# Query projections of a second self attention by sets of seven block products

## The chip, the cores and the metric

The kernel runs on one core of a Trainium2 chip. Its metric is the device time of one execution in microseconds (us). The kernel before took 1819.48 us, the median of three runs from 1816.45 to 1821.72. All data is 32-bit floating point.

The core has five engines that work beside each other: TensorE for matmuls (PE in the profile, its weight loads as PEld), VectorE (DVE), ScalarE (ACT), GpSimd (POOL) and SyncE (SP), which here only issues transfers. Matmul results land in PSUM banks; all other tiles lie in SBUF.

## The reference

The computation is a two-layer decoder over 8 sequences of 112 tokens with 512 features (896 tokens). Each layer has a self attention, a cross attention to a context of 375 tokens, and a feed-forward part, each on the layer norm of the running sum `x` and added to it. The change touches the self attention of the second layer:

```python
q = q * cos + _rotate_half(q) * sin
k = k * cos + _rotate_half(k) * sin
...
scores = jnp.einsum('bhqd,bhkd->bhqk', q, k) * scale
...
attn = jax.nn.softmax(scores, axis=-1)
out = jnp.einsum('bhqk,bhkd->bhqd', attn, v)
out = out.transpose(0, 2, 1, 3).reshape(b, s, H * DH)
return out @ Wo.T
```

Here `q = x @ Wq.T` has 16 heads of 128 features, `k` and `v` 4 heads, each used by four query heads. The positions run over each sequence's 112 tokens. The mask of this attention leaves out keys more than 128 positions ahead, which no pair here is.

## The kernel before, in words

`self_attention(1, ...)` works in eight turns, one for each pair of a key head group `g` (0 to 3) and a half `hf` of the tokens (448 tokens, four sequences). The input `xT[hf]` lies transposed: 128 features on the partitions, four chunks of features, 448 tokens. For each turn, `prepare(n)` gives a list of steps: the keys (`roped` with `wk`) and the four query heads of the group (`roped` with the group's 512x512 matrix `matrices[g][0]`). Each such head is four matmuls of 128x128 by 448 columns, which the profile shows as eight records, into one PSUM bank of the tag `mm`, which has two buffers.

`roped` then copies the bank to a tile `raw` (L630 on DVE, L632 on ACT in the first layer), has SP move its two halves of 64 rows crosswise into a tile `turned` (L637), multiplies `raw` by the cosine on POOL (L639) and `turned` by the sine on DVE (L640), and adds both on POOL into `qT` or `kT` (L641). `raw` and `turned` have three buffers each.

`scores` (L695) makes a unit's 16 score matmuls, `softmax` takes the maxima on DVE (L466), the exponentials on ACT (L469) and scales on POOL (L476); `contexts` transposes the result (L487, copied out by DVE at L488), multiplies it with the values (L714) and copies it to `oT` on ACT (L719). `pipeline` and `weave` set the order: while a turn's first unit is worked on, `weave` mixes in the next turn's keys and queries, then the output projection of the turn before (`outputs(n - 1, True)`); with the second unit it mixes in `outputs(n, False)` and then the steps of `extra(n)`. The order on PE is the written one; the other engines' instructions are ordered by a planner that keeps the dependencies and lets an instruction go early when its inputs are ready.

The output projection adds into `x`, which keeps tiles of 128 tokens. Where a turn completes two tiles and `g` is below 3, `out_pair` makes both together: the two tiles' tokens, the matrix's columns and the 512 inner features are each cut in two, and seven products of the 2x2 blocks (`sevens`, numbered 1, 6, 2 and 5, 7, 3, 4 in the order that PE makes them) take the place of eight. They need three sums of input blocks, made per pair by `block_sums` (L253 to L258, the tile `os`), and three differences of matrix blocks, made per matrix by `block_differences` (L267 to L272, the tile `wos`, and one in place in `wo`). The step `lay` in `prepare` makes the latter. One half of a seven uses two banks, and a product that adds to a bank waits until the engine that reads the bank has read the product before. The readers (`put`, L768 and L771 on DVE, L782 and L785 on POOL) keep three differences in a tile `od`. `os`, `od` and `wos` have one buffer each in a pool `dq`.

Weights come through the pool `wpool` of six buffers of 1 MB. The second layer's first two query matrices are fetched at the start, the third in `prepare(3)` and the fourth in `prepare(5)`.

## Time and profile before

The profile is of one execution that took 1820.96 us; its span, from the first to the last instruction, is 1819.0 us.

| engine | busy us | share of the span | instructions |
|---|---|---|---|
| PE | 1769.6 | 97% | 7150 |
| PEld | 989.8 | 54% | 7150 |
| DVE | 952.1 | 52% | 1692 |
| ACT | 627.5 | 34% | 1906 |
| POOL | 770.0 | 42% | 673 |

| in the second self attention, 930 to 1190 us | count | mean |
|---|---|---|
| query matmul record, 448 columns | 224 | 540 ns |
| output product record, 256 columns | 252 | 379 to 394 ns |
| DVE copy of a raw head (L630) | 35 | 625 ns |
| DVE sine product (L640) | 35 | 620 ns |
| POOL cosine product of a query head (L639) | 28 | 1439 ns |
| POOL sum of a query head (L641) | 29 | 1142 ns |
| DVE reader of an output product (L768) | 54 | 414 to 421 ns |

A record's duration of a matmul runs until its last result; the next one is issued before that. So the pace of PE is read from the distance of the starts, or from the chain of waits, and not from these means. In the timeline, the brackets give how long the engine stood idle before an instruction and what ended that. The chain of waits is followed back from the last instruction; a piece names the work that the end of the program hung on at that time.

### The profile page before, as it was taken

To read this page: it belongs to the slowest core of one execution; us is meant where nothing else is said; L and a number is where in the kernel's file an instruction comes from. 1 tells how busy PE (TensorE), PEld (TensorE's weight loads), DVE (VectorE), ACT (ScalarE), POOL (GpSimd) and SP (SyncE) were. 2 spreads that over 40 slices of the span, in tenths; PEclk is the share of its full clock that TensorE was granted. 3 is DMA by queue.
4 is the path that set the end of the run, shared out by engine and by line. 5 is a ranking of instruction groups with operands and counts; after the bars stand their busy time and mean duration, and the time that the engine had idled before them with its cause. 6 is when DMAs were issued, how large, how long until landed. Compare 5 with 4: busy or idle time off the path is not lost.

```text
span 1819.0 us, 20344 instructions
## 1 busy us (share of the span) xinstructions
PE 1769.6 (97%) x7150; PEld 989.8 (54%) x7150; DVE 952.1 (52%) x1692; ACT 627.5 (34%) x1906; POOL 770.0 (42%) x673
## 2 busy tenths in 40 slices
PE   8999999999999999999999999999999999999998
PEld 4454544555454555567655666645654444554444
DVE  4455666645454544786543545536755444344444
ACT  2444444554333434375221221236722111031110
POOL 3464555355656550000135666512353354434533
PEclk9999999999999999999999999999999999999999
DMA  6132423143133212011121222300011212011111
GB/s 242 27 118 64 143 82 89 58 150 115 48 85 101 58 52 93 24 70 63 63 66 33 75 77 44 104 18 1 8 37 53 75 55 81 23 50 55 63 34 41
DMA packets 40429, 124.50 MB, mean 68 GB/s; under 512 B 7332, under 2 KB 20700, under 8 KB 32904
## 3 DMA queue, kind: packets, MB, share of 16 engines
q1 hardware_dynamic: 33192, 93.73, 16.0%
q0 software_dynamic: 6848, 29.36, 5.4%
q8 instruction: 56, 0.92, 0.2%
q14 instruction: 45, 0.37, 0.1%
q10 hardware_dynamic: 288, 0.12, 0.0%
HBM read 94.56 MB, written 10.28 MB: 58 GB/s over the span
## 4 chain that ended last, share of the span: by engine, by line
PE 81%; DVE 8%; POOL 4%; ACT 3%; DMA 2%; issue 1%; SPq 1%; ACTq 0%; POOLq 0%; DVEq 0%
PE pr_q L244 10%; PE pf L244 5%; PE po_x L1004 4%; PE pb_dn L1550 4%; PE po_at L442 3%; PE pv L244 3%; PE po_at L446 3%; PE pr_k L244 3%; PE ps L695 3%; PE pq_x L244 3%; PE po L714 3%; PE po_x L442 2%; PE po_x L446 2%; PE pa_dn L1550 2%; PE ps_x L968 2%; PE pb_up L1550 2%
## 5 line engine op out<-in xcount | busy, mean ns | idle before, releaser
L244 PE MATMUL pr_q<-xT_at,wq 128*128 128x448 f32 x512 | 204.1, 543 | 0.0
L244 PEld LDWEIGHTS pr_q<-xT_at,wq 128*128 128x128 f32 x512 | 93.8, 190 | 84.3 <-issue 81.3
L469 ACT ACTIVATE p<-p,nmax 112x113 f32<-112x113 f32 x256 | 95.8, 376 | 109.7 <-DVE nmax L466 108.8
L1733 POOL TENSOR_TENSOR h<-silu,h 128x448 f32<-128x448 f32 x64 | 73.9, 1157 | 122.2 <-ACT silu L1731 122.0
L476 POOL TENSOR_TENSOR p<-p,total 112x896 f32<-112x896 f32 (+1 forms) x56 | 85.3, 1529 | 93.7 <-DVE total L472 86.5
L244 PE MATMUL pf<-h,sw 128*128 128x448 f32 x256 | 106.0, 540 | 0.0
L1127 POOL TENSOR_SCALAR tl<-tr,ternary_bounds 128x512 f32<-128x512 f32 x32 | 51.8, 1618 | 123.2 <-DMA tr<-in_c_w_dram 123.2
L1735 DVE TENSOR_TENSOR h<-h,share 128x448 f32<-128x448 f32 x48 | 41.5, 871 | 111.9 <-POOL h L1733 111.9
L974 DVE TENSOR_REDUCE nmax_x<-ps_x 112x2 f32<-112x750 f32 x64 | 57.1, 933 | 79.4 <-PE ps_x L968 79.4
L641 POOL TENSOR_TENSOR qT<-qT,turned_q 128x448 f32<-128x448 f32 x64 | 75.5, 1182 | 51.3 <-DVE turned_q L640 42.0
L639 POOL TENSOR_TENSOR qT<-raw_q,tables 128x448 f32<-128x448 f32 x64 | 85.1, 1334 | 27.9 <-DVE raw_q L630 20.4
L1004 PE MATMUL po_x<-pT_x,kv 125*128 125x448 f32 x192 | 89.2, 549 | 1.6 <-DVE pT_x L999 1.3
L976 ACT ACTIVATE p_x<-ps_x,nmax_x 112x375 f32<-112x375 f32 x124 | 69.7, 574 | 38.2 <-DVE nmax_x L974 38.1
L1550 PE MATMUL pb_dn<-h,sums_dn 128*128 128x448 f32 x192 | 80.3, 541 | 1.0 <-DVE acc L1772 0.5
L1731 ACT ACTIVATE silu<-pf,cols 128x448 f32<-128x448 f32 x64 | 40.5, 633 | 117.9 <-PE pf L244 117.0
L488 DVE COPY pT<-ppt 112x448 f32<-112x448 f32 x96 | 57.1, 617 | 43.5 <-PE ppt L487 43.5
L469 ACT ACTIVATE p<-ps,nmax 112x112 f32<-112x112 f32 x128 | 43.2, 366 | 101.7 <-DVE nmax L466 101.7
L244 PEld LDWEIGHTS pf<-h,sw 128*128 128x128 f32 x256 | 48.9, 191 | 48.2 <-issue 41.7
L442 PE MATMUL po_at<-wo,oT 128*128 128x512 f32 x152 | 74.3, 611 | 0.0
L446 PE MATMUL po_at<-wo,oT 128*128 128x512 f32 x152 | 71.4, 592 | 0.0
L719 ACT COPY oT<-po 128x448 f32<-128x448 f32 x64 | 31.9, 525 | 104.9 <-PE po L714 104.9
L476 POOL TENSOR_TENSOR p_e<-p_e,total_e 112x896 f32<-112x896 f32 x16 | 26.9, 1682 | 96.5 <-DVE total_e L472 72.2
(357 smaller groups left out, 3941.5 us busy)
## 6 DMA issues: line engine op xcount, KB each, us to landing
tw<-in_c_w_dram SPq DMA_DIRECT2D x16, 512.0 KB
tr<-in_c_w_dram POOLq DMA_DIRECT2D x32, 256.0 KB, 3.8
signs<-tl POOLq DMA_DIRECT2D x32, 256.0 KB, 2.9
fup<-in_f_up_dram SPq DMA_DIRECT2D x8, 1024.0 KB
fdn<-in_f_dn_dram SPq DMA_DIRECT2D x8, 1024.0 KB
turned_q<-raw_q SPq DMA_DIRECT2D x128, 56.0 KB
turned_q<-raw_q SPq DMA_DIRECT2D x64, 112.0 KB
share<-gated SPq DMA_DIRECT2D x12, 448.0 KB
```

The lines of the kernel that those rows point to most:

```text
L244: nc.tensor.matmul(ps, lhsT, rhs, start=(k == 0), stop=(k == len(pairs) - 1))
L442: nc.tensor.matmul(ps[0], lhsT, rhs, start=(c == 0), stop=False)
L446: nc.tensor.matmul(ps[0], lhsT, rhs, start=False, stop=(c == len(pairs) - 1))
L469: nc.scalar.activation(p[:, h, :], src[:, h, :], AF.Exp, bias=nmax[:, h : h + 1], accum_out=total[:, h : h + 1])
L476: spread[:] = [nc.gpsimd.tensor_tensor(p[:, at, :T], p[:, at, :T], total[:, at], ALU.mult).ins]
L488: copied[:] = [nc.vector.tensor_copy(kept["pT"][:, 4 * k : 4 * k + 4, :], pt[:T, :, :T]).ins]
L639: nc.gpsimd.tensor_tensor(by_batch(dst), by_batch(raw), cos, ALU.mult)
L641: nc.gpsimd.tensor_tensor(dst, dst, turned, ALU.add)
L976: e = nc.scalar.activation(p[:, 2 * j + s, :], ps[:T, s, :L], AF.Exp, bias=nmax[:, s : s + 1], accum_out=total[:, 2 * j + s : 2 * j + s + 1],)
L1004: nc.tensor.matmul(po[0][:, : 4 * T], kv[:, b, c, :], pTs[c], start=(c == 0), stop=(c == NLC - 1))
L1550: nc.tensor.matmul(bank[n], lhsT, rhs, start=(k == 0 and n in (1, 6, 7)), stop=(k == len(pairs) - 1), skip_group_check=True,)
L1733: nc.gpsimd.tensor_tensor(to, s, at["h1"][:, c, half(hf)], ALU.mult)
```

## The change

From the third turn on, the four query heads of a turn are made as two pairs, each by a set of seven products. The two heads of a pair are one cut, the halves of the 512 inner features the second, and two halves of 224 tokens the third. `paired` makes a pair in two steps. The three sums of matrix blocks, with one difference in place, are made per matrix (`add_up`, for matrices 1 to 3), the four differences of input blocks once per token half (`differ`); both are steps of `extra`: the first matrix's sums and the first half's differences in turn 0, the second half's in turn 1, the other matrices' in turns 2 and 4.

The end of `roped` becomes a function `rotated`, whose last add can go to DVE; the second head of the second pair uses that. The raw copies of the first two turns go to ACT. The output pairs' `os` and `od` move from `dq` to the three buffers of 512 columns with the tag `xn` in the pool of the normed inputs: the first two input sums in one buffer, the third sum and the first difference in another, the other two differences in the third. In `dq` their place is taken by `sums` (one buffer) and `xs0`, `xs1`.

```diff
@@ extra
-                return [(3.4, lambda b=b: values(b)) for b in range(first, last)]
+                steps = [(3.4, lambda b=b: values(b)) for b in range(first, last)]
+                if not l0 and n == 0:
+                    more = later(add_up(1) + differ(0))
+                    steps = [*more[:3], steps[0], *more[3:6], steps[1], *more[6:]]
+                return steps
             if not l0:
-                return []
+                g, hf = turns[n]
+                return later(differ(1) if n == 1 else add_up(g + 1) if hf == 0 and g + 1 < G else [])
@@ roped
-            if bias is None:
-                nc.vector.tensor_copy(raw, ps[:, :HT])
+            raw = new_raw(name)
+            if bias is None and name.startswith("k") and xs:
+                nc.vector.tensor_copy(raw, ps[:, :HT])
+            elif bias is None:
+                nc.scalar.copy(raw, ps[:, :HT])
...
+        def differ(hf):
+
+            b = xT[hf].rearrange("p (h k) (s t) -> p h k s t", h=2, s=2)
+
+            def new():
+                xs[hf] = dq[0].tile([P, 4, 2, HT // 2], F32, tag=f"xs{hf}", bufs=1, name=f"xs_{layer}_{hf}")
+
+            return block_differences(
+                (nc.vector, nc.gpsimd), new, lambda k: xs[hf][:, k],
+                b[:, 0, :, 0], b[:, 0, :, 1], b[:, 1, :, 0], b[:, 1, :, 1],
+            )
+
+        def add_up(g):
+
+            a = matrices[g][0].rearrange("p (h k) (c m n) -> p h k c m n", h=2, c=2, m=2)
+
+            def new():
+                sums[g] = dq[0].tile([P, 3, 2, 2, P], F32, tag="sums", bufs=1, name=f"sums_{layer}_{g}")
+
+            return block_sums(
+                (nc.vector, nc.gpsimd), new, lambda k: sums[g][:, k],
+                a[:, 0, :, :, 0], a[:, 1, :, :, 0], a[:, 0, :, :, 1], a[:, 1, :, :, 1],
+            )
+
+        def paired(turn, qT, c, nm):
...
+            def put(n, ps):
+                if n == 1:
+                    raw[:] = [new_raw(f"q_{nm}_{2 * c + m}") for m in range(2)]
+                r0, r1 = raw
+                add = lambda to, of: nc.vector.tensor_tensor(to, of, ps, ALU.add)
+                if n == 1:
+                    nc.vector.tensor_copy(r0[:, tok[1]], ps)
+                elif n == 6:
+                    add(r1[:, tok[0]], r0[:, tok[1]])
+                elif n == 2:
+                    nc.scalar.copy(r0[:, tok[0]], ps)
+                elif n == 5:
+                    add(r1[:, tok[1]], r1[:, tok[0]])
+                elif n == 7:
+                    add(r1[:, tok[1]], r1[:, tok[1]])
+                elif n == 3:
+                    add(r0[:, tok[1]], r1[:, tok[0]])
+                    rotated(qT[:, 2 * c, :], r0, "q", f"q_{nm}_{2 * c}")
+                else:
+                    add(r1[:, tok[0]], r1[:, tok[0]])
+                    rotated(qT[:, 2 * c + 1, :], r1, "q", f"q_{nm}_{2 * c + 1}", nc.vector if c else nc.gpsimd)
+
+            first, second = sevens(products, put, half_, f"q_{nm}_{c}", c == 1)
+            return [(2.3, first), (3.0, second)]
+
+        def rotated(dst, raw, which, name, last=nc.gpsimd):
...
-            nc.gpsimd.tensor_tensor(dst, dst, turned, ALU.add)
+            last.tensor_tensor(dst, dst, turned, ALU.add)
@@ prepare
-            more = later(lay(g - 1)) if not l0 and n and hf == 0 else []
-            for c in range(4):
-                steps += more[c : c + 1]
-                steps.append((3.0, lambda c=c: roped(
...
+            if l0 or n < 2:
+                for c in range(4):
+                    steps.append((3.0, lambda c=c: roped(
...
+            else:
+                more = [step for c in range(2) for step in paired(n, qT, c, nm)]
+                if hf == 0:
+                    more = [step for pair in zip(more, later(lay(g - 1))) for step in pair]
+                steps += more
@@ out_pair, add_up
-                    s.append(dq[0].tile([P, 3, 2, P], F32, tag="os", bufs=1, name=f"os_{nm}"))
+                    pair = [npool.tile([P, D], F32, tag="xn", bufs=3, name=f"os_{nm}_{k}") for k in range(2)]
+                    d.append(pair[1][:, D // 2 :])
+                    pair = [t.rearrange("p (s c n) -> p s c n", s=2, c=2) for t in pair]
+                    s.extend([pair[0][:, 0], pair[0][:, 1], pair[1][:, 0]])
...
@@ out_pair, put
-                    d.append(dq[0].tile([P, 3, D // 2], F32, tag="od", bufs=1, name=f"od_{nm}"))
-                d1, d2, d3 = (d[0][:, m] for m in range(3))
+                    d.append(npool.tile([P, D], F32, tag="xn", bufs=3, name=f"od_{nm}"))
+                d1, d2, d3 = d[0], d[1][:, : D // 2], d[1][:, D // 2 :]
```

## The prediction

> **What bounds the kernel now.** I read the page's busy times first, then the chain of waits cut to the second self attention (about 930 to 1190 us), then the timeline around each gap that the chain shows.
>
> ```profile
> PE 1769.6 (97%) x7150; PEld 989.8 (54%) x7150; DVE 952.1 (52%) x1692; ACT 627.5 (34%) x1906; POOL 770.0 (42%) x673
> ...
> PE 81%; DVE 8%; POOL 4%; ACT 3%; DMA 2%; issue 1%; SPq 1%; ACTq 0%; POOLq 0%; DVEq 0%
> ```
>
> PE is busy 97% of the span, and the chain runs through it. So a microsecond of matmul taken from this stage is worth one, unless PE then waits. One turn of the stage in the chain (start, length, what):
>
> ```profile
> 1055.46 3.02 PE pr_q L244 x8
> 1058.87 3.02 PE pr_q L244 x8
> 1061.89 1.50 PE po L714 x4
> 1063.40 3.01 PE pr_q L244 x8
> 1066.41 0.86 PE px_at_True L286 x4
> 1067.27 0.98 PE py_at_True L286 x4
> 1068.26 0.86 PE px_at_True L286 x4
> 1069.12 0.86 PE py_at_True L286 x4
> 1069.98 0.86 PE pz_at_True L286 x4
> ```
>
> A query head is eight records in 3.01 to 3.02 us, 377 ns each at 448 columns. The output sets are already made of seven products: four records of 256 columns in 0.86 us, 216 ns each. One product has 0.98, because its bank still waited for the raw copy of the last head. Busy time of the engines in such a stretch (window, length, PE, PEld, DVE, ACT, POOL):
>
> ```profile
> 1049.00:1072.00 23.00, 23.00 (x80) 13.69 (x79) 10.95 (x22) 3.76 (x18) 15.65 (x13) 1.00 0.33 83
> 1072.00:1085.00 13.00, 12.49 (x76) 10.36 (x75) 7.61 (x17) 3.76 (x18) 7.74 (x9) 1.00 0.25 104
> ```
>
> The clock is 1.00; DVE and POOL have room on the mean. The second stretch holds the one repeated gap, seen in the timeline (start, length, engine):
>
> ```profile
> 1005.94 1.09 DVE L466 TENSOR_REDUCE nmax<-ps 112x8 f32<-112x896 f32 x1 [0.46 <-PE ps L695]
> 1006.39 1.26 POOL L785 TENSOR_TENSOR x<-x,od_at_True 128x512 f32<-128x512 f32 x1
> 1006.62 1.03 PE L286 MATMUL py_at_False<-wos,os_at_False 128*128 128x256 f32 x4
> ...
> 1007.68 0.42 DVE L771 COPY od_at_False<-px_at_False 128x256 f32<-128x256 f32 x1 [0.65 <-PE py_at_False L286]
> 1008.16 1.13 PE L286 MATMUL px_at_False<-wo,oT 128*128 128x256 f32 x4 [0.52 <-DVE od_at_False L771]
> ```
>
> PE should have gone on at 1006.62 + 0.865 = 1007.48 and starts at 1008.16. DVE was free from 1007.03, yet the copy into od started only when POOL's L785, which reads the previous od tile, ended at 1007.65.
>
> **The change, part by part.**
>
> *Shorter products.* Six turns have two head pairs each: 12 pairs. A pair was 16 records, 16 x 0.377 = 6.03 us. It becomes seven products of two matmuls, 28 records of 224 columns. From 377 ns at 448 and 216 ns at 256 columns the slope is 0.839 ns a column, so 224 columns take 189 ns: 28 x 0.189 = 5.30 us. That is -0.73 a pair, **-8.8 us**. The weight load (190 ns as shown) should not stand in the way: the score matmuls of 112 columns go 16 in 1.57 us, 98 ns each, each with its own load of 112 columns.
>
> *Bank wait gone.* The pair ends with a reader of 224 columns in place of one of 448. DVE copies out of PSUM took 0.625 us at 448 and 0.424 at 256, so 0.39 at 224. The 0.12 us in the first py product of the six late output pairs goes: **-0.7 us** (ends 0 and -0.7).
>
> *The output sets move into the xn buffers.* The first difference now lies in the tile of the third input sum, no longer in the tile that L785 reads. The copy can start when nmax ends, 1007.03, ends at 1007.45, and PE starts near 1007.5. Next in line is then nmax itself, which just fits. The gap of 0.68 us comes three times: up to -2.0, at worst 0; I take **-1.6**.
>
> *Waits inside the new sevens.* A product's reader starts 0.20 us after its last record has been issued (998.87 to 999.07), runs 0.39, and PE follows 0.05 later: 0.64 us. The one product between covers 0.757. The margin is 0.12 us, where the output sets had 0.865 - 0.67 = 0.20. Laid out over one turn from the end of the key matmuls: the key's rotated half lands near 3.8 us, so its sine product (0.62) falls between the readers of products 5 and 7, and product 4 starts some 0.15 late. The pT copies (0.62 each) meet the gap behind a half set. The sine products of the first pair fall into the 1.5 us of po between the halves of the second. A raw buffer is reused at the sixth product of the second pair, 0.5 us before its transfer out has ended; DVE waits there, but PE has product 2 and po ahead of the next bank it needs. Ends: 0, as in the late output pairs apart from the bank wait, and 0.68 a seven, the worst repeated gap. I take 0.25, nearer to the first, since that is the same scheme: 12 x 0.25 = **+3.0** (0 to +8.2). DVE gets, per pair, six readers for two copies, 6 x 0.39 - 2 x 0.625 = +1.1 us, and in every second pair the last add (0.62): +2.8 us a turn on 10.95 of 23. POOL loses one add of 1.13 a turn, ACT gains two short copies in a time when its exponentials are over.
>
> The Trainium skill, "SBUF — State Buffer", section "Who interferes with whom", speaks against the new DVE work: a DVE instruction with both inputs in SBUF and a GpSimd one that reads SBUF exclude each other for a whole instruction. The trace agrees in part: wos L271 took 1.65 us beside POOL's L785 against 0.66 where it started first, but the sine products stayed at 0.62 while POOL ran. By the rule alone 18 new instructions of that kind (6 of the differences, 6 sums, 6 adds) could each wait about 1 us; were all on the path, that would be +18 us.
>
> *Input differences and the first sums.* They are ready from about 926 us on. DVE stands idle 2.34, 1.61 and 3.76 us in 932 to 944, which hides them (8 instructions of about 0.65, and four on POOL); if one comes earlier, POOL may be in a sum of 1.27 us (the row of L270) when the first scores wait for qT at 928.83. Ends 0 and +1.3; I take **+0.4**.
>
> *Sums of the third and fourth matrix.* Each has two DVE instructions (0.68, or 1.65 beside POOL) and two of 1.27 on POOL. They must follow the last product that uses the sums before, so they fall beside the late output pair, where the gaps of DVE are 0.44. Ends 0 and 1.65 each; I take 0.4 each, **+0.8**. The matrix itself is fetched at 1000.11, 40 us before: no wait.
>
> *Ten raw copies on ACT.* Around 910.5 a raw copy holds DVE 0.53 us ahead of rest_h, on the chain; on ACT it would stand before top_h instead. Ends -0.5 and +0.6; I take **-0.2**.
>
> *Last heads into the scores.* Both heads of the second pair come out within 0.8 us. The later one: reader, transfer (2.96 us in the row at 1030.18 to 1033.14), sine product 0.62, add on DVE 0.62, about 4.9 us after the last product. The output pair behind it runs 6.1, so 1.2 is left (0.1 today): **0**. With no output pair behind it, it would cost all of 4.9. SP's queue carries the same count of transfers, the two of a pair closer together.
>
> Sum: -8.8 - 0.7 - 1.6 + 3.0 + 0.4 + 0.8 - 0.2 = **-7.1 us**. The profiled execution took 1820.96 us (span 1819.0), which would be 1813.9; it stands 1.5 above the median of 1819.48. I carry the difference to the median: 1812.4 us.
>
> The Trainium skill, "VectorE: DVE Perf Modes", section on the errata of SBUF-source operations, asks for pieces of 512 elements or more, since each instruction pays a fixed cost. Here the fixed part is 0.625 - 448 x 1.05 ns = 0.155 us in the rows; by it the cut into 224 costs 12 x 4 x 0.155 = 7.4 us of DVE, which would end the gain only if DVE were the bound.
>
> **The rivals.**
>
> *A. The readers eat the gain.* Every new seven loses what the early output pair loses now, 0.68 us: 12 x 0.68 = 8.2 in place of 3.0, so -7.1 + 5.2 = -1.9: 1817.6 us. For it: the margin of 0.12. Against it: in the late output pairs DVE kept step with a sine product in between.
>
> *B. Slower: DVE sets the pace of the sevens.* A two-input SBUF instruction held by POOL (1.65 us) or a wait for a rotated half (2.40 us of DVE idle at 1063.16 to 1065.56) stands ahead of a reader in each seven. The other terms sum to -10.1, so B decides from 10.1 / 12 = 0.84 us a seven; at 1.65 less the margin, 1.5, it gives -10.1 + 18 = +8: 1827 us. Against it: the sine products are not stretched by POOL (at most 0.77 us), and that DVE wait had nothing ready behind it.
>
> *C. The products don't get shorter.* If a record of 224 columns took the 216 ns of one of 256, a pair would be 6.05 us, no gain, and the sum -7.1 + 9.0 = +1.9: 1821.4 us. Against it: the 98 ns records.
>
> **How the numbers follow.** About 0.3% (5.5 us) is what a measurement of this kernel can tell from no change: faster is below 1814.0, slower above 1824.9. Forecast 0.60, its own range 1807.5 (all good ends: -12.0) to 1815.5; A 0.26; B 0.11; C 0.03. A part of the forecast's case (0.04) lies above 1814.0, and a bit of A (0.02) below: faster 0.58; with C and 0.01 of B same 0.32, slower 0.10. The range 1808 to 1820.5 leaves out some 0.06 below and 0.12 above.
>
> **What would show it.** The chain after: query products of four records in about 0.76 us, seven of them in 5.3 to 5.6 us a pair; the first py product of the late output pair at 0.86; px_at_False following its neighbour without a DVE piece of od. The DVE busy time rises by about 17 us. The forecast is wrong if PE rows of the new sevens carry idle time ended by DVE of more than 0.8 us a pair, if the scores wait longer than 2.3 us for qT at 930, or if the records of 224 columns come slower than 200 ns.

## The result, and where the time went

The changed kernel takes 1824.22 us (median of 20 runs, 1820.45 to 1830.28); the kernel before, timed beside it, 1820.21 us. The ratio is 1.0023, 95% interval 1.0015 to 1.0031: slower by some 4.2 us. That is inside the 5.5 us which the prediction called no change, but on the other side of its forecast of 7.1 us gained, and 3.7 us above the upper end of its range. The profiled execution took 1822.7 us (span 1820.9).

Busy times and the chain of waits after the change, the lines that answer to the first ones of before:

```profile
PE 1763.4 (97%) x7294; PEld 1012.4 (56%) x7294; DVE 983.0 (54%) x1748; ACT 636.8 (35%) x1928; POOL 767.3 (42%) x675
...
PE 78%; DVE 9%; POOL 3%; ACT 3%; DMA 3%; issue 2%; SPq 1%; DVEq 0%; ACTq 0%; POOLq 0%
```

TensorE has 6.2 us less to do, and its part of the chain falls from 81% to 78%. What it lost there went to VectorE, transfers and issue. The two stretches whose busy times were shown of before (window, length, PE, PEld, DVE, ACT, POOL, TensorE's clock, DMA share, GB/s):

```profile
1053.10:1077.20 24.10, 22.38 (x105) 17.79 (x104) 15.53 (x31) 4.45 (x20) 14.71 (x14) 1.00 0.36 91
1077.20:1090.20 13.00, 13.00 (x78) 10.73 (x77) 7.69 (x18) 3.76 (x18) 7.41 (x8) 1.00 0.20 83
```

The first stretch holds two of the new sevens. It should have become shorter than 23.00 us and is 24.10, with TensorE idle for 1.7; VectorE is busy for 15.53 us in place of 10.95, 1.8 us more than the rise of 2.8 that the prediction counted for a turn. The second stretch has lost its gap: 12.49 busy of 13.00 became 13.00 of 13.00.

The timeline of the same turn and of its neighbour (start, length, engine, line; in brackets the idle time before and what ended it):

```profile
1032.84 1.13 POOL L723 TENSOR_TENSOR qT<-qT,turned_q 128x448 f32<-128x448 f32 x1 [2.57 <-DVE turned_q L722]
1032.91 1.53 DVE L722 TENSOR_TENSOR turned_q<-turned_q,tables 128x448 f32<-128x448 f32 x1
...
1034.37 0.38 DVE L690 TENSOR_TENSOR raw_q<-raw_q,py_q 128x224 f32<-128x224 f32 x1
...
1034.80 1.02 PE L286 MATMUL py_q<-xT_at,sums 128*128 128x224 f32 x4 [0.72 <-DVE raw_q L690]
...
1061.32 0.62 DVE L722 TENSOR_TENSOR turned_k<-turned_k,tables 128x448 f32<-128x448 f32 x1 [0.97 <-DMA turned_k<-raw_k]
1061.86 0.38 DVE L690 TENSOR_TENSOR raw_q<-raw_q,pz_q 128x224 f32<-128x224 f32 x1
...
1062.15 0.38 DVE L690 TENSOR_TENSOR raw_q<-raw_q,py_q 128x224 f32<-128x224 f32 x1
1062.29 1.02 PE L286 MATMUL pz_q<-xs,wq 128*128 128x224 f32 x4 [0.86 <-DVE raw_q L690]
...
1067.39 0.92 PE L286 MATMUL py_q<-xs,sums 128*128 128x224 f32 x4
...
1068.15 0.92 PE L286 MATMUL pz_q<-xs,wq 128*128 128x224 f32 x4
...
1068.91 0.92 PE L286 MATMUL py_q<-xT_at,sums 128*128 128x224 f32 x4
...
1069.66 0.92 PE L286 MATMUL pz_q<-xs,wq 128*128 128x224 f32 x4
...
1070.42 1.03 PE L286 MATMUL px_at_True<-wo,oT 128*128 128x256 f32 x4
...
1074.30 1.13 POOL L723 TENSOR_TENSOR qT<-qT,turned_q 128x448 f32<-128x448 f32 x1 [1.67 <-DVE turned_q L722]
...
1074.42 1.30 DVE L253 TENSOR_TENSOR os_at_False<-oT 128x256 f32<-128x256 f32 x1
...
1075.63 0.61 DVE L722 TENSOR_TENSOR turned_q<-turned_q,tables 128x448 f32<-128x448 f32 x1
...
1076.17 0.41 DVE L857 TENSOR_TENSOR od_at_True<-od_at_True,pz_at_True 128x256 f32<-128x256 f32 x1
...
1076.63 1.13 PE L286 MATMUL pz_at_True<-wos,oT 128*128 128x256 f32 x4 [0.87 <-DVE od_at_True L857]
```

Three things are to be seen. From 1067.39 to 1070.42 four products follow each other in 0.76 us each: where nothing stands in front of its readers, a new seven runs as forecast. At 1062.29 and at 1034.80 TensorE waits for a reader, because VectorE had stood still for a rotated half (0.97 us), or had spent 1.53 us on a sine product that takes 0.62 alone. At 1076.63 it waits in the output set: its reader stands behind a first input sum of 1.30 us and, after that, a sine product of 0.61. At 1034.80 and 1076.63 the long VectorE instruction started 0.07 and 0.12 us after a GpSimd add of 1.13 us, and ended 0.5 and 0.3 us after its end.

The waits from 890 to 1190 us (engine, line, waited for, us in total, times, longest):

```profile
PE pz_at_True L286 <- DVE od_at_True L857: 4.0, 6, 0.9
PE ps L781 <- POOL qT L723: 3.3, 1, 3.3
PE pz_q L286 <- DVE raw_q L690: 2.2, 2, 1.4
PE po_ff L1334 <- DVE rest_h L1232: 1.8, 2, 1.2
PE px_at_True L286 <- DVE os_at_True L860: 0.9, 2, 0.4
PE py_q L286 <- DVE raw_q L690: 0.7, 1, 0.7
```

In the text below, a gap is the start of a group of matmuls less the end of the group ahead, that end being its start and its records at their pitch (189 ns at 224 columns, 216 at 256, 377 at 448, 98 at 112). By that measure the gaps from 981 to 1190 us were 2.9 us before and are 13.5 now. From the stage's first key matmul to the first query matmul of the cross attention behind it, it took 319.86 us before and takes 323.75 now. That difference of 3.9 us is nearly the whole loss, and it falls into three parts:

| part of the stage | measured | the prediction's terms |
|---|---|---|
| start, up to the second turn's scores | +2.0 | +0.2 |
| six stretches with two new sevens each | +4.1 | -8.8 - 0.7 + 3.0 + 0.8 = -5.7 |
| three early output pairs | -2.2 | -1.6 |

### The profile page after: what moved, and what is told of

Its sections match the earlier page's. It is cut to its first block, busy times and chain, and to the rows that moved or that the text cites. A ratio compares the mean times of both kernels' runs of the same rounds, so it can differ in the third digit from the quotient of the medians.

```text
span 1820.9 us, 20781 instructions
## 1 busy us (share of the span) xinstructions
PE 1763.4 (97%) x7294; PEld 1012.4 (56%) x7294; DVE 983.0 (54%) x1748; ACT 636.8 (35%) x1928; POOL 767.3 (42%) x675
## 4 chain that ended last, share of the span: by engine, by line
PE 78%; DVE 9%; POOL 3%; ACT 3%; DMA 3%; issue 2%; SPq 1%; DVEq 0%; ACTq 0%; POOLq 0%
PE pr_q L244 6%; PE pf L244 5%; PE po_x L1093 4%; PE pb_dn L1639 4%; PE po_at L442 3%; PE po_at L446 3%; PE pv L244 3%; PE ps L781 3%; PE pr_k L244 3%; PE pq_x L244 3%; PE po_x L442 2%; PE po L800 2%; PE po_x L446 2%; PE pa_dn L1639 2%; PE ps_x L1057 2%; PE pb_up L1639 2%
## 5 line engine op out<-in xcount | busy, mean ns | idle before, releaser
L244 PE MATMUL pr_q<-xT_at,wq 128*128 128x448 f32 x320 | 127.9, 545 | 0.0
L723 POOL TENSOR_TENSOR qT<-qT,turned_q 128x448 f32<-128x448 f32 x58 | 69.6, 1203 | 46.2 <-DVE turned_q L722 39.4
L244 PEld LDWEIGHTS pr_q<-xT_at,wq 128*128 128x128 f32 x320 | 58.3, 190 | 53.2 <-issue 50.0
L721 POOL TENSOR_TENSOR qT<-raw_q,tables 128x448 f32<-128x448 f32 x64 | 77.3, 1218 | 24.7 <-ACT raw_q L637 11.5
L1084 PEld LDWEIGHTS ppt_x<-consts,p_x 112*125 112x125 f32 x372 | 50.2, 188 | 29.6 <-issue 15.5
```

The source lines that it names most:

```text
L244: nc.tensor.matmul(ps, lhsT, rhs, start=(k == 0), stop=(k == len(pairs) - 1))
L721: nc.gpsimd.tensor_tensor(by_batch(dst), by_batch(raw), cos, ALU.mult)
L723: last.tensor_tensor(dst, dst, turned, ALU.add)
```

## The experiments

Each experiment is compared with the kernel before, timed beside it. "Stage" is the difference in the length just described, from one profiled execution each.

**The output sets' move alone, and the two engines swapped.** The first kernel keeps only the move into the xn buffers; all queries are made by whole heads, without sums and differences for them, and the raw copies are on VectorE:

```diff
-            if bias is None and name.startswith("k") and xs:
+            if bias is None:
                 nc.vector.tensor_copy(raw, ps[:, :HT])
-            elif bias is None:
-                nc.scalar.copy(raw, ps[:, :HT])
...
-            if l0 or n < 2:
+            if True:
```

> Only the move of the output sets' os and od into the xn buffers; queries, raw copies and weights as before. Both theories: the gap of 0.68 us in front of px_at_False (three times) goes, -2.0 us. Theory 1 (the loss lies in what DVE does ahead of a reader): the first sum of the next output pair (L253) is no longer held back by a buffer and is put ahead of a reader of the late pair, so that the last pz product of turns 1, 3 and 5 waits up to 0.4 us: total about -1 us against before, 1819. Theory 2 (the loss lies in the short margin of the new products themselves): no new wait, -2 us.

Measured: 1818.27 us, ratio 0.9987 (0.9975 to 0.9998). The three gaps of 0.68 us at px_at_False are gone, 0.7 us less in each of those three pairs, and no gap came at pz_at_True. So this term of the sum holds by itself. The first input sum of the early pair went early here too, started 0.12 us behind a GpSimd add and took 1.29 us; but the late pair's reader that TensorE waits for had been done before it, so the long sum cost nothing. A stretched instruction harms only with an urgent reader behind it.

The second kernel gives the cosine product to VectorE and the sine product to GpSimd, so that, but for head 3's last add, no VectorE instruction hangs on a transfer:

```diff
-            nc.gpsimd.tensor_tensor(by_batch(dst), by_batch(raw), cos, ALU.mult)
-            nc.vector.tensor_tensor(by_batch(turned), by_batch(turned), sin, ALU.mult)
+            early_, late_ = (nc.gpsimd, nc.vector) if l0 else (nc.vector, nc.gpsimd)
+            early_.tensor_tensor(by_batch(dst), by_batch(raw), cos, ALU.mult)
+            late_.tensor_tensor(by_batch(turned), by_batch(turned), sin, ALU.mult)
```

> The changed kernel, but in the second layer DVE multiplies by the cosine and GpSimd by the sine, so that nothing on DVE waits for a rotated half, except the last add of the fourth head. Theory 1: the gaps ended by DVE raw_q in the second halves of the sets (0.98, 1.02, 1.52 us in the trace of after) fall below 0.2, and those of pz_at_True from 1.0 to about 0.5: -4 to -6 us against the changed kernel, about 1819. Theory 2: the gaps stay, since the readers themselves are too slow: within 1 us of the changed kernel, 1823 to 1825. A third outcome: GpSimd, which now waits for the transfers, is late with the scaled probabilities, and PE waits at ppt or po.

Measured: 1841.31 us, ratio 1.0121 (1.0106 to 1.0137). The three gaps of 0.98, 1.02 and 1.52 us inside the second halves are gone; gaps of 0.2 to 0.5 us came in both pairs of all six turns, and the output pair lost 2.7 us six times: head 3's last add is VectorE's, and it stood ahead of a reader, waiting for a sine product that GpSimd now made late. It moved the wait to a worse place and settled nothing about its cause.

**The start, and the early pair's sums.** The third kernel puts the raw copies of the first two turns back on VectorE, and holds the first sums and differences behind the second unit's maxima and scaled probabilities:

```diff
-            if bias is None and name.startswith("k") and xs:
+            if bias is None:
                 nc.vector.tensor_copy(raw, ps[:, :HT])
-            elif bias is None:
-                nc.scalar.copy(raw, ps[:, :HT])
...
+                    def behind_first(f):
+                        with tc.issue_after(marks[0]), tc.issue_after(marks[1]):
+                            f()
```

> The changed kernel, but the raw copies of the first two turns back on DVE, and the first sums and input differences held behind the second unit's maxima (DVE) and scaled probabilities (GpSimd). Theory 1 for the start: the two losses between the first key matmuls and the first scores go, 0.95 us near 911 (the normalisation stretched from 1.00 to 1.82 us by GpSimd's earlier cosine product) and 1.0 us near 930 (GpSimd's difference of the weights ahead of the last sum of qT): -1.9 us, about 1822. Rival: the start is a shift that comes from elsewhere, and the first scores stay as late, 38.1 us after the first key matmul.

Measured: 1821.46 us, ratio 1.0007 (0.9996 to 1.0017), stage +1.6 in place of +3.9. The start is as before: the scores wait 2.30 us for qT again, not 3.30. In the changed kernel GpSimd's first difference of the matrix had run ahead of the add that the scores wait for:

```profile
930.61 1.58 POOL L256 TENSOR_TENSOR wq<-wq 128x512 f32<-128x512 f32 x1 [1.09 <-DVE sums L253]
...
932.15 1.57 POOL L723 TENSOR_TENSOR qT<-qT,turned_q 128x448 f32<-128x448 f32 x1
...
933.78 2.22 PE L781 MATMUL ps<-kT,qT 128*112 128x112 f32 x20 [3.30 <-POOL qT L723]
```

The other microsecond was a wait of 1.27 us for rest_h at 914.12, 0.30 before. It is missing in the next kernel, which still has the raw copies on ACT, so it belongs to that one execution or comes only sometimes; the two halves of this edit were not run apart.

The fourth kernel is the changed one with the input sums of each output pair held behind the last reader of the pair before:

```diff
+                    with tc.issue_after(read[0]) if read else nullcontext():
                         step()
```

> The changed kernel, but an output pair's input sums stand on DVE behind the last reader of the output pair before. Theory 1: pz_at_True in turns 1, 3 and 5 then waits as in turn 6, where no such sum stands there, 0.70 in place of 1.02 us: -1 us in all, 1823. If the sum alone were the cause, the three gaps would go, -3 us, 1821.

Measured: 1822.2 us, ratio 1.0018 (1.0009 to 1.0027). The three gaps of 1.02 us at pz_at_True became 0.70, and three new ones of 0.44 came at px_at_False. The sum of 1.30 us was a part of the gap; what remains of it has other work in front.

**Moving work behind the readers.** The next three build on the third kernel (1821.46 us; gaps of 1.04, 0.66, 1.03, 0.65, 1.04 and 0.71 at pz_at_True, 0.64 twice at px_at_True, 0.99, 0.72 and 1.30 in the second halves).

```diff
-                return later(differ(1) if n == 1 else add_up(g + 1) if hf == 0 and g + 1 < G else [])
+                def behind_reader(f):
+                    with tc.issue_after(read[0]):
+                        f()
+
+                if n > 1 and hf == 0 and g + 1 < G:
+                    return [(0.0, lambda f=f: behind_reader(f)) for f in add_up(g + 1)]
+                return later(differ(1) if n == 1 else [])
```

> On top of the kernel with the early start mended (raw copies of the first two turns on VectorE, first sums and differences behind the second unit's maxima; 1821.46 us), the sums of the third and fourth query matrix are held behind the last reader of the late output pair. Theory 1 (the order on VectorE: a two-input instruction that is free early is put ahead of a reader that TensorE's next product needs, and takes 1.3 us where GpSimd works beside it): the two gaps of 0.64 us at px_at_True go and the gaps of 0.66 us at pz_at_True in the same two turns fall to 0.3 or less, in sum -2.0 us: 1819.5. Theory 2 (VectorE has too little room in these stretches as a whole, so that work moved back only pushes the next work): the gaps come again at the scores or the first product behind them, 1821 to 1822.

Measured: 1822.23 us, ratio 1.0015 (1.0006 to 1.0025). The two gaps of 0.64 went, those of 0.65 stayed at 0.70, and 0.4 us at po and 0.7 at the scores behind came new, in both turns. Theory 2's outcome. The sixth holds back the sine product and the add of the key and of heads 0 and 1:

```diff
+            def finish():
+                nc.vector.tensor_tensor(by_batch(turned), by_batch(turned), sin, ALU.mult)
+                last.tensor_tensor(dst, dst, turned, ALU.add)
+
+            if held_back:
+                owed.append(finish)
+            else:
+                finish()
...
+        def pay(reader):
+            with tc.issue_after(reader.ins):
+                owed.pop(0)()
```

> Same base (1821.46 us), but VectorE's sine products of the key and of the first head pair are held back: the key's behind the last reader of the first pair, head 0's behind the reader of product 7 of the second pair, head 1's behind its last reader. Nothing else moves. Theory 1 (a sine product waits for its transfer, or is stretched by GpSimd, with a reader behind it in VectorE's order): the gaps of 0.99, 0.72 and 1.30 us in the second halves go, -3.0 us: 1818.5. Theory 2 (no room on VectorE): the sine products now fall beside the output pair and add what they save to the gaps at pz_at_True (0.65 to 1.04 us now, 1.2 to 1.6 then): 1821 to 1823.

Measured: 1824.92 us, ratio 1.0031 (1.0018 to 1.0043). The three waits in the second halves went. In their place came 0.56 us six times at the third product of the second pair, behind the key's sine product, in three turns pz_at_True waits 1.7 us, and in the two turns with matrix sums the first output products wait 0.85, 0.54 and 0.70. Theory 2 again.

The seventh has both edits, and the early pair's sums held behind the reader of product 3 of the late one:

```diff
+                    with tc.issue_after(third[0]) if third else nullcontext():
                         step()
```

> Both of these, and the first sum of the early output pair held behind the reader of product 3 of the late pair. Theory 1: of 14.1 us of gaps 3.0 (second halves), 1.3 (px_at_True) and some 3.5 of the 5.1 at pz_at_True go, 0.4 to 1.3 come new at px_at_False: 1814 to 1816, faster than both kernels. Theory 2: 1819 or more.

Measured: 1822.28 us, ratio 1.0015 (1.0005 to 1.0024). The stretches with two new sevens take as long as before the change (0 to 0.4 us more each), the early pairs keep their gain of 0.7, pz_at_True is down to 0.48 six times; but two turns lose 1.8 us each where the sums went. The timeline of one of them:

```profile
1038.80 0.92 DVE L253 TENSOR_TENSOR sums<-wq 128x512 f32<-128x512 f32 x1
1039.13 1.72 POOL L907 TENSOR_TENSOR x<-x,od_at_True 128x512 f32<-128x512 f32 x1
...
1039.64 1.75 DVE L267 TENSOR_TENSOR wos<-wo 128x512 f32<-128x512 f32 x1
...
1040.81 1.71 POOL L256 TENSOR_TENSOR wq<-wq 128x512 f32<-128x512 f32 x1
...
1041.32 1.75 DVE L257 TENSOR_TENSOR sums<-sums,wq 128x512 f32<-128x512 f32 x1
...
1042.99 1.08 DVE L467 TENSOR_REDUCE nmax<-ps 112x8 f32<-112x896 f32 x1
```

VectorE's instructions and GpSimd's take turns: 0.68 becomes 1.75 and 1.26 becomes 1.7, and VectorE's end 0.5 us after GpSimd's. They put the maxima at 1042.99, though TensorE had done the scores at 1039.48. Moved work meets the other engine again in its new place.

**Order refined, and two prices.** The eighth kernel changes three places of the seventh: the matrix sums wait for the maxima, the key's and head 0's sine products go into the stretch of po, head 1's behind the reader of product 3.

```diff
-                    with tc.issue_after(read[0]):
+                    with tc.issue_after(maxima[-1]):
...
                 elif n == 6:
-                    add(r1[:, tok[0]], r0[:, tok[1]])
+                    reader = add(r1[:, tok[0]], r0[:, tok[1]])
+                    if c:
+                        pay(reader)
+                        pay(reader)
```

> The kernel with the held sums and sine products once more, with three places changed by what its trace showed. The matrix sums wait for the next unit's maxima only, so that they no longer stand ahead of them (0.96 and 0.79 us of gaps in two turns, 3.5 in sum). The sine products of the key and of head 0 stand behind the second reader of the second pair, where the matmuls of po leave VectorE idle, and no longer ahead of that pair's first reader (0.56 us six times). Head 1's stands behind the reader of product 3, so that its last add on GpSimd goes ahead of the cosine products of heads 2 and 3 (0.48 us six times at pz_at_True). Theory 1 (the order decides, there is room): 15.3 us of gaps become 6 to 8, 1822.3 becomes 1814 to 1816. Theory 2 (VectorE and GpSimd have no room for these products in this stretch): 1819 or more, with the gaps at other products.

Measured: 1818.22 us, ratio 0.9990 (0.9979 to 1.0001). The gaps of 0.56 at the third product are gone, but pz_at_True waits 0.79 us six times: head 3's sine product took 1.49 us, from 0.12 after the start of GpSimd's add for head 2. Neither theory's number: 4.5 us better than the seventh (1.0015 to 0.9990), and not shown to be faster than before.

The ninth kernel prices the sine products (base: the third kernel); it returns ahead of the sine product and the add:

```diff
+            if not l0 and name.startswith("q") and name[2:] >= "1_1_0":
+                return
             nc.vector.tensor_tensor(by_batch(turned), by_batch(turned), sin, ALU.mult)
             last.tensor_tensor(dst, dst, turned, ALU.add)
```

> The early-start base (1821.46 us) without the sine products and the adds behind them for the 24 heads of the third turn on: the heads are left as their cosine products alone, so this part of the computation is left out; transfers and cosine products stay. It prices them. Theory 1 (these instructions and their lock with GpSimd make the waits of the new sevens): the gaps at pz_at_True (5.1 us) and in the second halves (3.0 us, except where the key's sine product is the one in front, 0.7 to 1.3 each in two turns) go, and 1821.5 becomes 1814 to 1816. Theory 2 (the products of 224 columns are too short for their own readers): nothing but the part of the sine product itself goes, 1819 or more.

Measured: 1814.34 us, ratio 0.9960 (0.9947 to 0.9974). Against the third kernel that is 0.0047 of the time, or 8.5 us, with an uncertainty of some 3. The gaps at pz_at_True are 0.08 us or less. The readers by themselves keep step with products of 224 columns, so the prediction's first rival, in which they do not, is out. What stays is 0.64 twice from the matrix sums, and 0.36, 0.73 and 0.79 where the key's sine product is in front.

The tenth kernel keeps all of VectorE's instructions and takes GpSimd's cosine products and adds of the same 24 heads away:

```diff
+            if not l0 and name.startswith("q") and name[2:] >= "1_1_0":
+                nc.vector.tensor_tensor(by_batch(dst), by_batch(turned), sin, ALU.mult)
+                if last is nc.vector:
+                    last.tensor_tensor(dst, dst, turned, ALU.add)
+                return
```

> The early-start base (1821.46 us, 15.2 us of gaps in the stage) with all of VectorE's work kept, the 24 sine products and the six last adds too, but without GpSimd's cosine products and adds for those 24 heads: the cosine terms of these heads are left out of the computation, the sine product writes the head. It parts the two readings of the run without sine products (1814.34 us). Theory L (GpSimd's instructions stretch VectorE's: the sine products of the 24 heads took 854 ns in the changed kernel and 619 before, the first sums of the early output pair 1296 and 437, the last adds 914): the sine products come back to some 620 ns, the sums to 440, the gaps of 1.04 and 0.65 to 0.71 us at pz_at_True fall to 0.3 or less, 1816 to 1817.5; what waits for transfers (0.72 to 1.3 us in two turns) stays. Theory R (VectorE has no room for so many instructions beside seven readers, lock or not): the gaps at pz_at_True stay at 0.5 us or more each, 1820 to 1821.5.

Measured: 1815.78 us, ratio 0.9980 (0.9970 to 0.9990), 0.0027 or 4.9 us below the third kernel, with an uncertainty of some 2.5. The gaps at pz_at_True fall from 1.04 and 0.65 to 0.16 us or none; 0.99 stays twice at px_at_True and 0.99 and 1.44 where the key's transfer is waited for. The same instructions on VectorE cost little when GpSimd is away. That is theory L, for the gaps at pz_at_True. The rows, grouped by form from 980 to 1190 us (count, busy us, mean ns, idle before). Before:

```profile
L640 DVE TENSOR_TENSOR turned_q<-turned_q,tables 128x448 f32<-128x448 f32 x24 | 14.9, 619 | 15.8 <-DMA turned_q<-raw_q 15.8
...
L253 DVE TENSOR_TENSOR os_at_False<-oT 128x256 f32<-128x256 f32 x3 | 1.3, 437 | 0.0
```

The changed kernel:

```profile
L722 DVE TENSOR_TENSOR turned_q<-turned_q,tables 128x448 f32<-128x448 f32 x24 | 20.5, 854 | 8.3 <-DMA turned_q<-raw_q 8.2
...
L723 DVE TENSOR_TENSOR qT<-qT,turned_q 128x448 f32<-128x448 f32 x6 | 5.5, 914 | 0.0
...
L253 DVE TENSOR_TENSOR os_at_False<-oT 128x256 f32<-128x256 f32 x3 | 3.9, 1296 | 0.0
```

The tenth kernel, without GpSimd's part:

```profile
L727 DVE TENSOR_TENSOR qT<-turned_q,tables 128x448 f32<-128x448 f32 x24 | 14.9, 622 | 8.2 <-DMA turned_q<-raw_q 8.1
...
L729 DVE TENSOR_TENSOR qT<-qT,turned_q 128x448 f32<-128x448 f32 x6 | 4.3, 719 | 0.0
...
L253 DVE TENSOR_TENSOR os_at_False<-oT 128x256 f32<-128x256 f32 x3 | 1.3, 418 | 0.0
```

854 ns fall back to 622, 1296 to 418; the adds come from 914 to 719. On these three rows the changed kernel spends 20.5 + 5.5 + 3.9 = 29.9 us, the tenth 20.5.

**A version built on that.** The eleventh kernel is the eighth, but gives head 2's add to VectorE as well, and makes the sums of the third and fourth matrix on GpSimd alone, behind its last add of the output pair:

```diff
-                (nc.vector, nc.gpsimd), new, lambda k: sums[g][:, k],
+                (nc.vector if g == 1 else nc.gpsimd, nc.gpsimd), new, lambda k: sums[g][:, k],
...
-                    rotated(qT[:, 2 * c, :], r0, "q", f"q_{nm}_{2 * c}", held_back=not c)
+                    rotated(
+                        qT[:, 2 * c, :], r0, "q", f"q_{nm}_{2 * c}", nc.vector if c else nc.gpsimd, held_back=not c,
+                    )
```

> The last kernel with held sine products (1818.22 us, 0.79 us of gap at pz_at_True six times, 0.80 and 0.87 us in two turns from the sums) with two more changes: the add of head 2 is VectorE's as head 3's is, since GpSimd's add of 1.13 us held head 3's sine product for 1.49 us; and the sums of the third and fourth matrix are all GpSimd's, behind its last add of the late output pair. Theory L (what stretches is the lock between the two engines): the gap at pz_at_True falls from 0.79 to 0.2 us (-3.5 us) and the 1.67 us in two turns go (-3.3), 1818.2 becomes 1811.5 to 1813.5. Theory R (room on VectorE): the add of 0.62 us more makes the gap 0.9 us or more or moves it to the scores, 1817 to 1819.

Measured: 1819.39 us, ratio 0.9996 (0.9987 to 1.0004). The gap at pz_at_True fell from 0.79 to 0.45, the sine products to a mean of 699 ns, but 0.76 and 0.80 us stayed in two turns: the sums of the late pair (1.42 and 1.79 us beside GpSimd) stood ahead of the maxima, and with them ahead of the key's raw copy. In the profile these two places give 2.3 of the 6.8 us that theory L asked for, and the timing shows no gain over the eighth.

The twelfth moves those sums behind the maxima, gives head 1's add to VectorE, and puts head 2's behind the reader of product 7:

```diff
-                    with tc.issue_after(third[0]) if third else nullcontext():
+                    with tc.issue_after(maxima[-1] if nm.endswith("True") else third[0]) if third else nullcontext():
                         step()
...
-                        qT[:, 2 * c + 1, :], r1, "q", f"q_{nm}_{2 * c + 1}", nc.vector if c else nc.gpsimd,
+                        qT[:, 2 * c + 1, :], r1, "q", f"q_{nm}_{2 * c + 1}", nc.vector,
...
+            elif not l0 and name.startswith("q") and name.endswith("_2") and len(xs) > 1:
+                nc.vector.tensor_tensor(by_batch(turned), by_batch(turned), sin, ALU.mult)
+                adds.append(lambda: last.tensor_tensor(dst, dst, turned, ALU.add))
```

> The last kernel (1819.39 us; 13.2 us of gaps in the stage, of them 0.45 us six times at pz_at_True and 0.76 and 0.80 us in two turns behind the key) with every add of the second head pair on VectorE, head 2's behind the reader of product 7 of the output pair, and with the sums of the late output pair behind the maxima that they stood in front of. GpSimd then has nothing but cosine products beside the second pair and the output pair. Theory L (the lock between VectorE and GpSimd makes the gaps): the reader of product 7 is no longer late, 0.45 becomes 0.1 six times, the maxima and the key's copy come in time, -2.1 and -2.5 us: 1814 to 1816, faster than both kernels. Theory R (room on VectorE): twelve more instructions of 0.61 us on VectorE cost as much as they save, 1818 to 1821.

Measured: 1814.96 us, ratio 0.9976 (0.9966 to 0.9985): faster than the kernel before by 4.4 us, and than the changed one by some 8.5. Its stage is 5.0 us shorter than before. The output pair of one turn in its timeline:

```profile
1001.34 0.62 DVE L749 TENSOR_TENSOR turned_q<-turned_q,tables 128x448 f32<-128x448 f32 x1
1001.87 0.41 DVE L899 TENSOR_TENSOR od_at_True<-od_at_True,pz_at_True 128x256 f32<-128x256 f32 x1
1002.20 0.62 DVE L750 TENSOR_TENSOR qT<-qT,turned_q 128x448 f32<-128x448 f32 x1
1002.34 1.13 PE L286 MATMUL pz_at_True<-wos,oT 128*128 128x256 f32 x4 [0.19 <-DVE od_at_True L899]
```

Sine product, reader and add stand in a row at their undisturbed lengths, and TensorE waits 0.19 us at the product where it waited 0.87 in the changed kernel. What is left in the turn is 0.51 us at the third product of the output pair, where head 1's add, 1.26 us beside GpSimd's cosine products, stands ahead of the first reader. VectorE's busy time over the whole kernel is 985.1 us, more than the 983.0 of the changed kernel, with 18 instructions more: it was not the amount of work. The three edits were not run apart, so what each is worth stays open; head 1's add on VectorE brings the 0.5 us just named in each of the six turns. And of the 9.5 us that the prediction's two gains in the six stretches would give, the twelfth kernel has 2.7: so much shorter these stretches are than before.

| kernel | ratio to before | stage, us |
|---|---|---|
| the change | 1.0023 | +3.9 |
| output sets' move alone | 0.9987 | -0.2 * |
| engines swapped | 1.0121 | +23.3 * |
| start mended | 1.0007 | +1.6 |
| change, input sums held | 1.0018 | +4.7 * |
| start, matrix sums held | 1.0015 | +3.3 |
| start, sine products held | 1.0031 | +8.7 * |
| both and the early sum | 1.0015 | +2.1 |
| order refined | 0.9990 | +2.5 * |
| start, no sine products | 0.9960 | -3.8 * |
| start, no GpSimd part | 0.9980 | -2.0 * |
| head 2's add, sums on GpSimd | 0.9996 | -0.2 * |
| head 1's add, sums behind the maxima | 0.9976 | -5.0 |

In the rows with a star the profiled execution has a dip of TensorE's clock near 930 us, told of below, which makes some 1.6 us of the stage.

## Why the prediction was wrong, step by step

*Shorter products* (-8.8): right. Products of four records come every 0.76 us where nothing holds them, which is the 189 ns a record that it said. The rival in which they do not get shorter is out.

*Bank wait gone* (-0.7): right, but given back. The first py product of the late pair follows after 0.86 us. In its place the first two products behind the key's raw copy come 0.12 and 0.10 us late in each of six turns, 1.3 us that the sum did not have.

*Output sets into xn buffers* (-1.6): right, -2.2 measured. "Next in line" was named as the maxima; the work that was freed as well, the next pair's first sum, went ahead of a reader, and with GpSimd beside it cost 0.3 us three times.

*Waits inside the new sevens* (+3.0) and *Last heads into the scores* (0): these are the steps that failed. The six stretches took 4.1 us more, where -9.5 for the two gains in them would have been: 13.6 us of waits, against 3.8 in the sum with the matrix sums counted in. Some 5 of them stand between the products of the new sevens, 0.4 a seven where 0.25 was taken; 1.3 of these are the products behind the key's copy. The larger part, some 6.8, stands in the late output pairs that follow: 5.1 at pz_at_True, 1.3 at px_at_True, 0.4 at py_at_True. The prediction followed the last two heads as far as the scores, found 1.2 us to spare and put 0. That is right as it was put, for no scores but the first wait for qT. But what covered the reader, transfer, sine product and add of these heads was the output pair, and they fell between its readers; that had no price in the sum.

So rival B's mechanism is what came: a two-input instruction held by GpSimd, or a wait for a rotated half, ahead of a reader. It came at less than B's 1.5 us a seven, and mostly not in the sevens, where B had put it. Of the three signs by which the prediction would have known itself wrong, the wait of the scores for qT came (3.30 us); the two that look at the query products did not, and none looked at the output pair. VectorE's busy time rose by 30.9 us where about 17 was said; 5.6 of that lie in the longer sine products alone (20.5 us against 14.9 in the rows above).

The fault that the two steps share lies in one sentence, "the sine products stayed at 0.62 while POOL ran". The rows of before show how it was misread:

```profile
1059.13 0.62 DVE L640 TENSOR_TENSOR turned_q<-turned_q,tables 128x448 f32<-128x448 f32 x1
...
1059.30 1.44 POOL L639 TENSOR_TENSOR qT<-raw_q,tables 128x448 f32<-128x448 f32 x1 [0.35 <-DVE raw_q L630]
```

The sine product was not disturbed here, and had started first; GpSimd's cosine product behind it took 1.44 us in place of 1.13. The price was there, paid by an engine that had time for it. Before, heads came out 3.0 us or more apart, so that one head's add was over before the next head's sine product began. The sets of seven bring a pair's heads out 0.75 us apart: both sine products become ready together, the second starts just behind GpSimd's add for the first, and the one that pays is VectorE, with a reader behind it. The Trainium skill, "SBUF — State Buffer", section "Who interferes with whom", says just this: of a VectorE instruction with two SBUF inputs and a GpSimd one that reads SBUF, whichever starts first has the shared ports for its whole length and the other is blocked. The 1.53 us against 0.62, and the return to 622 ns in the tenth kernel, agree. Five rows of before do not, as far as their starts tell: the first head's cosine product began 0.37 us ahead of the key's sine product, and yet it was the long one.

```profile
1055.89 1.97 POOL L639 TENSOR_TENSOR qT<-raw_q,tables 128x448 f32<-128x448 f32 x1 [0.30 <-DVE raw_q L630]
...
1056.26 0.61 DVE L640 TENSOR_TENSOR turned_k<-turned_k,tables 128x448 f32<-128x448 f32 x1
```

No run here explains these five. The prediction weighed the rule and put it aside on the wrong rows: GpSimd's rows, beside the same sine products, show the loser.

How the 13.6 us divide is shown in part. Taking GpSimd's part away gains 4.9 us, taking the sine products and adds away gains 8.5. In the tenth kernel some 8 us of gaps stay: 2.0 behind the matrix sums, which both engines still make, 2.4 where the key's transfer is waited for, 1.3 behind the key's copy, and small ones. So the lock is shown for about 5 us, the gaps at pz_at_True; the wait for the key's transfer is there without it. Moving work alone brought little: over their base of 1.0007 the fifth to seventh kernels gained nothing, the eighth 3.1 us, and the twelfth, in which VectorE makes the adds of heads 1 to 3 and the order is changed again, 5.6.

*Sums of the third and fourth matrix* (+0.8): too small. Two gaps of 0.64 us stay even without the sine products, and held behind the output pair the sums cost 1.2 us a turn in the fifth kernel and 1.8 in the seventh.

*Input differences and the first sums* (+0.4): +1.0 in the profile, by just the case that was named for the upper end: GpSimd was in a sum when the scores waited for qT. *Ten raw copies on ACT* (-0.2): not settled, nothing or +1.0. Both together, mended in the third kernel, give 0.0016 of the time, 2.9 us with an uncertainty of some 2.4.

So the sum of -7.1 became +3.9 by 1.8 us at the start and 9.8 in the six stretches, less 0.6 at the early pairs.

## What to carry to other kernels

When two engines share a lock, an undisturbed row on one proves nothing: look at what the other's row beside it took, and ask which of the two will be the long one, and what stands behind it, once the change has moved them. A forecast that follows a late result to its consumer must also price the instructions that it passes on the way. A scheme that hands over two results at once, where they came one by one, makes the second one's work collide with the first one's. The kernel that was faster in the end gave both steps of most results to one engine, the busier one, and placed them between its readers; which of its edits did it was not shown.

## What the runs showed that was not expected

TensorE's clock drops for a few microseconds in some executions and not in others of kernels that are the same at that place. After a wait of 2.30 us for qT, some 930 us in, the eighth kernel's clock (the first figure behind the engines' busy times) fell:

```profile
928.00:930.00 2.00, 1.88 (x10) 1.88 (x11) 1.40 (x2) 0.14 (x1) 0.07 (x1) 0.55 0.00 0
930.00:932.00 2.00, 2.00 (x13) 1.98 (x13) 0.76 (x3) 1.66 (x10) 0.00 (x0) 0.60 0.04 8
```

and the third kernel's, with the same wait, did not:

```profile
931.00:933.00 2.00, 1.60 (x16) 1.60 (x17) 1.81 (x2) 0.42 (x1) 0.35 (x1) 1.00 0.00 0
```

The dip is there in eight of the fourteen profiles, five of the ten with a wait of 2.30 us and three of the four with a longer one. In the eighth kernel it makes the stretch from the first scores to the values 1.6 us longer. There are other dips in some profiles, most often near 330, 1250, 1345, 1390 and 1580 us; those near 1345 and 1580 lie behind rows of matmuls of 8 columns, through which TensorE counts as busy. The Trainium skill, "TensorE: Matmul & The Clock Gate", section "What's actually happening", has the array at half its clock after an idle window of some 3.4 us that runs freely; the half clock agrees, and a free window would explain why it strikes only sometimes, but here 2.30 us of waiting were enough, and no run tested it. By that page a window at half the clock loses 1.7 us, an estimate near the 1.6 seen. A difference of that size between two single profiles is no effect of an edit: the profile of the kernel that moved the output sets alone has 2.3 us less of gaps, and its stage is only 0.2 us shorter.
